# Softmax exponentials head by head from PSUM, with the scaled maximum as the bias

## The chip, the cores and the metric

The kernel runs on one core of a Trainium2 chip. The metric is the device time of one execution in microseconds (us); lower is better. The engines are called as the profile calls them: PE (TensorE), with PEld for its weight loads, DVE (VectorE), ACT (ScalarE), POOL (GpSimd) and SP (SyncE, which issues most of the transfers).

## The reference

The computation is a gated cross-attention block followed by a gated feed-forward block. There are 2 x 2048 rows of 512 numbers; each row attends to 77 context rows of its batch, with 16 heads of 32 numbers.

```python
x = x + tanh(g_xattn) * attention(layernorm(x), ctx)
x = x + tanh(g_ffn) * ffn(layernorm(x))
# attention, per head:
scores = q @ k.T / sqrt(32)              # 77 scores for each row
attn = softmax(scores, axis=-1)          # exp(scores - max) / sum
out = concat(attn @ v) @ Wo.T + bo
# ffn: two linear layers, each with its input and weight rounded to 127 levels
# by the largest absolute value of the whole tensor; an exact gelu between them
```

The change is inside the softmax: the largest of the 77 scores is taken from each of them, and the exponential is taken with the scale 1/sqrt(32).

## The kernel before, in words

The 4096 rows are cut into 8 blocks of 512 rows (index i). A block is worked on in 8 steps (index s), so attention has 64 steps, k = 8i + s. One step handles one group of four heads (g = s // 2) for two tiles of 128 rows; odd steps take the second pair of tiles. A step therefore owns 2 tiles x 4 heads x 77 = 616 scores in each of 128 partitions.

The stages of a step's softmax are these:

- `scores` (L342): eight matmuls write the 616 scores into the PSUM tile `ps` (two buffers). Each multiplies `qT`, the projected queries, with `kb`, the keys. DVE takes the maximum of each head's 77 scores into `mx` (L361), and subtracts it, from PSUM into the SBUF tile `e` (L363; three buffers).
- `exponential` (L371): one ACTIVATE on ACT, in place on the 616 numbers of `e` (L373).
- `shares` (L375): DVE sums each head (`sm`, L380) and inverts the sum (`rs`, L382); POOL multiplies `e` by it (L384).
- `transpose_a` (L388): PE transposes `e` into the PSUM tile `pta` (L395), and ACT copies it out as `aT` (L396).

Other work lies around it. `apply_v` (L398) multiplies with the values: PE writes `pc` (L404), ACT copies it to `cT` (L412). `project_q` (L329) makes the next queries: PE writes `pq` (L332), ACT makes `qT` from it (L340). `project_o` makes the output product `po` (L420), and DVE adds it to `x` (L430). `pq`, `pc`, `po` and a few others share two PSUM buffers (tag `pp`). DVE also takes the statistics of rows (L163, L164 and `ve`, L170) and maxima of normalised rows (L196, L445). POOL turns variances into `rstd` (L171), scales `xT` (L289) and adds the output bias to `x` (L327).

Preparation of the feed-forward weights is spread over the attention steps: maxima on DVE (`max_w`, L465) in steps 4 to 11 and 21 to 28; rounding on ACT (`raw_w`, L481) in steps 13, 15, 17, 19, 31, 32, 36 and 40; conversion on DVE (`w1q` and `w2q`, L489) one step after each.

In attention, the order on PE, DVE and ACT is exactly the order in which the program is written. In step k, PE does `apply_v` (even steps), the scores of step k + 2, the transposes of step k, then `project_o` (even) or `project_q` (odd). ACT does `cT` (even), two `aT` copies, the exponential of step k + 2, `qT` (odd), and then weight rounding. DVE does the output addition (odd), `mx` and the subtraction of step k + 2, row maxima or statistics (mostly even steps), `sm` and `rs` of step k + 2, further statistics (odd) and weight work. The core of the loop reads:

```python
if ahead[0] < NB:
    scores(*ahead)
for u in range(2):
    transpose_a(i, s, u)
...
if ahead[0] < NB:
    last = exponential(*ahead)
...
if ahead[0] < NB:
    last = shares(*ahead)
```

After attention comes a feed-forward part: gelu on ACT from the PSUM tile `ph` (L738, L746), and the second product `pf` (L805).

Of the kernel before, what the change touches and what calls it, by code (L numbers as in the profile page):

```python
# [8 lines left out]
F32 = mybir.dt.float32  # L9
BF16 = mybir.dt.bfloat16  # L10
AF = mybir.ActivationFunctionType
ALU = mybir.AluOpType
# [3 lines left out]
P = 128  # L16
# [4 lines left out]
NK = 77  # L21
HG = P // DK
NG = HEADS // HG
GK = HG * NK
RT = 2
NR = HG // RT
# [12 lines left out]
SCALE = float(DK) ** -0.5  # L39
# [3 lines left out]
def tile_flamingo_gated_block(  # L43
# [21 lines left out]
    nc = tc.nc  # L65
# [6 lines left out]
    small = ctx.enter_context(tc.tile_pool(name="small", bufs=4))  # L72
# [25 lines left out]
    work = actx.enter_context(tc.tile_pool(name="work", bufs=2))  # L98
# [106 lines left out]
    def quantize(dst, src, inv):  # L205

        nc.vector.tensor_scalar(src, src, inv, MAGIC, ALU.mult, ALU.add)
        return nc.vector.tensor_scalar(dst, src, MAGIC, None, ALU.subtract).ins  # L208
# [5 lines left out]
    with actx:  # L214
# [43 lines left out]

        rstd_row, po = {}, {}
        ALL = slice(0, D)  # L260
        ln, xnT, qT, aT, cT, es = {}, {}, {}, {}, {}, {}

        def norm_stats(i, t):

# [77 lines left out]
        def scores(i, s):  # L342

            g, half = divmod(s, 2)
            n = f"{i}_{s}"

            ps = ps_s.tile([P, NR, 512], F32, tag="ps", name=f"ps{n}")
            for u in range(2):
                t = 2 * half + u
                for q in range(NR):  # L350
                    r = slice(q * RT * DK, (q + 1) * RT * DK)
                    nc.tensor.matmul(  # L352
                        ps[:, q, u * RK : (u + 1) * RK],
                        qT[i, g][r, t * P : (t + 1) * P],
                        kblk[i // NBB][r, g, :],
                        start=True,
                        stop=True,
                    )
            mx = small.tile([P, NR, 2, RT], F32, tag="mx", name=f"mx{n}")
            sc = ps[:, :, : 2 * RK].rearrange("p q (u r k) -> p q u r k", u=2, r=RT)  # L360
            nc.vector.tensor_reduce(mx, sc, AX.X, ALU.max)  # L361
            e = work.tile([P, 2, GK], F32, tag="e", name=f"e{n}", bufs=3)
            nc.vector.tensor_tensor(  # L363
                e.rearrange("p u (q r k) -> p q u r k", q=NR, r=RT),
                sc,
                mx[:, :, :, :, None].to_broadcast([P, NR, 2, RT, NK]),
                ALU.subtract,
            )
            es[i, s] = e

        def exponential(i, s):  # L371
            e = es[i, s]
            return nc.scalar.activation(e, e, AF.Exp, scale=SCALE).ins  # L373

        def shares(i, s):  # L375

            n = f"{i}_{s}"
            e4 = es[i, s].rearrange("p u (j k) -> p u j k", j=HG)
            sm = small.tile([P, 2, HG], F32, tag="sm", name=f"sm{n}")
            nc.vector.tensor_reduce(sm, e4, AX.X, ALU.add)  # L380
            rs = small.tile([P, 2, HG], F32, tag="rs", name=f"rs{n}")
            nc.vector.reciprocal(rs, sm)  # L382
            es[i, s] = e4
            return nc.gpsimd.tensor_tensor(  # L384
                e4, e4, rs[:, :, :, None].to_broadcast([P, 2, HG, NK]), ALU.mult
            ).ins
# [152 lines left out]
        for s in range(2):  # L539
            scores(0, s)  # L540
            exponential(0, s)
# [4 lines left out]
        for i in range(NB):  # L546
            more = i + 1 < NB
            for s in range(2 * NG):
                g, odd = divmod(s, 2)
                k = i * 2 * NG + s  # L550
# [6 lines left out]
                if ahead[0] < NB:  # L557
                    scores(*ahead)
# [4 lines left out]
                if ahead[0] < NB:  # L563
                    last = exponential(*ahead)
# [22 lines left out]
                if ahead[0] < NB:  # L587
                    last = shares(*ahead)
# [44 lines left out]
        i, last = NB - 1, range(NG - 1, NG)  # L633
# [35 lines left out]
        for kc in range(0, KC, 2):  # L669
# [3 lines left out]
            last = nc.vector.tensor_scalar(xqT0[:, kc + 1, :], v, MAGIC, None, ALU.subtract).ins  # L673
# [23 lines left out]
    with ExitStack() as fctx:  # L697
# [23 lines left out]
        for i in range(NB):  # L721
# [4 lines left out]
            for a in range(GT):  # L726
                G = gtile(f"G{i}_{a}")
                for v in range(GF // 2):
# [16 lines left out]
                    for u, fc in chunks:  # L745
# [4 lines left out]
                            bias=b1s[:, fc : fc + 1],  # L750
                            scale=s1,
                        )
                    k = (i * GT + a) * 2 + v
                    n = 1 if k == NB * GT * 2 - 1 else 2
# [24 lines left out]
    for i in ends:  # L779
        hq = hpool.tile([P, FC, TB], BF16, tag="hq", name=f"hq{i}")  # L780
        for a in range(GT):
# [6 lines left out]
            if (i, a) == (first, 0):  # L788
                with tc.manual_schedule(engines={mybir.EngineType.DVE}):
                    for v in range(GF):  # L790
                        last = quantize(dst[:, v, :], G[:, v, :], inv_h)
# [25 lines left out]
        for t in range(NT):  # L817
# [3 lines left out]
            n = 2 if i == ends[-1] and t == NT - 1 else 1  # L821
            for j in range(n):
# [7 lines left out]
                r = i * TB + t * P  # L830
# [64 lines left out]
```

## Time and profile before

| what | value |
|---|---|
| median of 3 runs | 638.99 us (638.86 to 639.27) |
| the profiled execution | 640.32 us |
| its span on the core | 638.5 us |
| PE busy | 615.9 us, 96% of the span |
| DVE busy | 509.0 us, 80% |
| ACT busy | 341.0 us, 53% |
| POOL busy | 247.2 us, 39% |
| first scores on PE | 20.6 us after the start of the span |
| last attention exponential on ACT | 376.3 us |
| first feed-forward matmul | 404.9 us |

The span is the time between the first and the last instruction in the trace, and the execution's own time has some 1.8 us more around it. All durations below come from that one profiled execution. Busy shares are averages over parts with different limits, so they have to be read again for each part. Matmuls overlap in PE, so a busy PE isn't by itself a PE at its peak.

### The profile page before, as it was taken

The numbers are of one execution on the slowest core, as the hardware profiler recorded it, in microseconds if no ns is written. First come the engines' busy times: TensorE is split into PE (matmuls) and PEld (weight loads), VectorE is DVE, ScalarE is ACT, GpSimd is POOL, SyncE is SP. The second block draws the span as 40 slices with busy tenths as digits, with TensorE's granted clock in tenths as the row PEclk, the third lists the DMA queues.
The fourth block names the chain that finished last, engine by engine and source line by source line (L and its number), as shares of the span: only waits on it lengthen the run. The fifth ranks groups of instructions, "written<-read, shape, count | busy, mean of one in ns | idle before, by whom it ended". The sixth has DMA issues, their size and how long they took to land.

```text
span 638.5 us, 8087 instructions
## 1 busy us (share of the span) xinstructions
PE 615.9 (96%) x2957; PEld 311.5 (49%) x2978; DVE 509.0 (80%) x796; ACT 341.0 (53%) x450; POOL 247.2 (39%) x202
## 2 busy tenths in 40 slices
PE   5999999999999999999999999799999979999997
PEld 5556555455545554555545555344444424444444
DVE  5688777889898997887857787899999789877452
ACT  2255444563434654544344442598989879556510
POOL 2145457465355364273362341000000009998000
PEclk9999999999999999999999999799999989999999
DMA  9921510442520232220000000199999109798932
GB/s 282 371 97 52 119 42 26 114 168 78 136 66 1 84 131 67 82 68 2 16 1 1 1 17 0 51 337 302 346 331 294 20 24 380 271 376 315 399 129 82
DMA packets 50542, 90.66 MB, mean 142 GB/s; under 512 B 22139, under 2 KB 26491, under 8 KB 44872
## 3 DMA queue, kind: packets, MB, share of 16 engines
q1 hardware_dynamic: 49400, 89.48, 42.8%
q10 hardware_dynamic: 1104, 0.69, 0.4%
q8 instruction: 23, 0.38, 0.2%
q14 instruction: 15, 0.12, 0.1%
HBM read 55.01 MB, written 31.47 MB: 135 GB/s over the span
## 4 chain that ended last, share of the span: by engine, by line
PE 81%; DVE 15%; ACT 1%; POOL 1%; issue 1%; DMA 1%; DVEq 0%
PE ph L738 17%; PE pf L805 17%; PE po L420 13%; PE pq L332 13%; PE pta L395 8%; PE ps L352 6%; PE pc L404 4%; DVE e L363 2%; DVE mx L361 2%; DVE sm L380 1%; DVE st_a L163 1%; DVE max_w L465 1%; PE pk L226 1%; DVE xmax L445 1%; PE pvv L250 1%; DVE x L430 1%
## 5 line engine op out<-in xcount | busy, mean ns | idle before, releaser
L384 POOL TENSOR_TENSOR e<-e,rs 128x616 f32<-128x616 f32 x64 | 81.7, 1277 | 164.4 <-DVE rs L382 77.2
L396 ACT COPY aT<-pta 77x512 f32<-77x512 f32 x128 | 68.2, 583 | 99.4 <-PE pta L395 99.4
L420 PE MATMUL po<-wo_sb,cT 128*128 128x512 f32 (+1 forms) x264 | 115.1, 580 | 0.0
L805 PE MATMUL pf<-w2q,hq 128*128 128x512 bf16 (+1 forms) x518 | 112.0, 376 | 2.9 <-DVE hq L208 2.1
L738 PE MATMUL ph<-xqT,w1q 128*128 128x512 bf16 x501 | 112.0, 383 | 2.6 <-DVE xqT L208 1.8
L746 ACT ACTIVATE G<-ph,b1s,s 128x512 f32<-128x512 f32 x128 | 99.4, 777 | 13.8 <-PE ph L738 2.9
L332 PE MATMUL pq<-xT,wq_sb 128*128 128x512 f32 x192 | 86.6, 593 | 0.2 <-POOL xT L289 0.2
L756 DVE TENSOR_REDUCE hmax<-G 128x1 f32<-128x1024 f32 (+1 forms) x65 | 77.0, 1198 | 7.2 <-ACT G L746 7.1
L805 PEld LDWEIGHTS <-hq 128*128 128x128 bf16 x528 | 51.9, 99 | 62.9 <-DVE hq L208 3.0
L738 PEld LDWEIGHTS <-w1q 128*128 128x128 bf16 x512 | 50.6, 99 | 63.9 <-issue 4.9
L380 DVE TENSOR_REDUCE sm<-e 128x8 f32<-128x616 f32 x64 | 50.3, 787 | 25.9 <-ACT e L373 25.9
L420 PEld LDWEIGHTS po<-wo_sb,cT 128*128 128x128 f32 x264 | 47.8, 190 | 47.5 <-issue 46.2
L395 PE MATMUL pta<-ident,e 128*77 128x128 f32 x512 | 70.2, 280 | 0.6 <-POOL e L384 0.6
L373 ACT ACTIVATE e<-e 128x616 f32<-128x616 f32 x64 | 45.9, 718 | 44.2 <-DVE e L363 42.0
L361 DVE TENSOR_REDUCE mx<-ps 128x8 f32<-128x616 f32 x64 | 50.6, 791 | 17.2 <-PE ps L352 16.9
L395 PEld LDWEIGHTS pta<-ident,e 128*77 128x77 f32 x512 | 55.6, 147 | 11.4 <-issue 9.4
L798 ACT ACTIVATE Gb<-Gb,inv_h 128x2048 f32<-128x2048 f32 x22 | 43.6, 1999 | 32.4 <-DMA Gb<-h 32.4
L352 PEld LDWEIGHTS ps<-kb,qT 64*128 64x128 f32 x512 | 36.0, 186 | 46.9 <-ACT qT L340 23.1
L819 POOL TENSOR_TENSOR x<-x,b_sb 128x512 f32<-128x512 f32 x32 | 57.2, 1823 | 0.1
L363 DVE TENSOR_TENSOR e<-ps,mx 128x616 f32<-128x616 f32 x64 | 51.2, 800 | 6.7 <-DVE mx L361 0.5
L332 PEld LDWEIGHTS pq<-xT,wq_sb 128*128 128x128 f32 x192 | 34.5, 190 | 35.0 <-issue 33.5
L827 DVE SCALAR_TENSOR_TENSOR x<-pf,s,x 128x512 f32<-128x512 f32 (+1 forms) x33 | 23.7, 730 | 34.4 <-PE pf L805 28.4
(101 smaller groups left out, 666.2 us busy)
## 6 DMA issues: line engine op xcount, KB each, us to landing
h<-G SPq DMA_DIRECT2D x22, 1024.0 KB, 6.0
Gb<-h SPq DMA_DIRECT2D x22, 1024.0 KB, 7.9
out_y<-x SPq DMA_DIRECT2D x31, 256.0 KB, 3.2
x<-in_x SPq DMA_DIRECT2D x7, 1024.0 KB, 7.4
xT<-in_xT SPq DMA_DIRECT2D x6, 1024.0 KB, 5.5
raw_w<-in_w2T SPq DMA_DIRECT2D x6, 1024.0 KB, 5.5
raw_w<-in_w1T SPq DMA_DIRECT2D x4, 1024.0 KB, 12.5
rrow<-row SPq DMA_DIRECT2D x6, 256.0 KB, 4.8
```

The source lines that it names most:

```text
L332: nc.tensor.matmul(pq, wq_sb[:, kc, g * P : (g + 1) * P], (xnT if i < 2 else xT_sb)[i][:, kc, :], start=(kc == 0), stop=(kc == KC - 1),)
L352: nc.tensor.matmul(ps[:, q, u * RK : (u + 1) * RK], qT[i, g][r, t * P : (t + 1) * P], kblk[i // NBB][r, g, :], start=True, stop=True,)
L361: nc.vector.tensor_reduce(mx, sc, AX.X, ALU.max)
L363: nc.vector.tensor_tensor(e.rearrange("p u (q r k) -> p q u r k", q=NR, r=RT), sc, mx[:, :, :, :, None].to_broadcast([P, NR, 2, RT, NK]), ...
L384: return nc.gpsimd.tensor_tensor(e4, e4, rs[:, :, :, None].to_broadcast([P, 2, HG, NK]), ALU.mult).ins
L395: nc.tensor.transpose(pt[:NK, j, :], es[i, s][:, u, j, :], ident)
L396: nc.scalar.copy(aT[i, g][:, :, t * P : (t + 1) * P], pt[:NK, :, :])
L420: nc.tensor.matmul(po[i, t, c.start][:, : c.stop - c.start], cT[i, g][:, t * P : (t + 1) * P], wo_sb[:, g, c], start=(g == 0), stop=(g == ...
L738: nc.tensor.matmul(ph[u], w1q[:, kc, fc * P : (fc + 1) * P], cur[:, kc, :], start=(kc == 0), stop=(kc == KC - 1),)
L746: nc.scalar.activation(G[:, 2 * v + u, :], ph[u], AF.Gelu, bias=b1s[:, fc : fc + 1], scale=s1,)
L756: nc.vector.tensor_reduce(hmax[:, k + u : k + u + 1], G[:, 2 * v + u : 2 * v + u + n, :], AX.XY, ALU.max, apply_absolute_value=True,)
L805: nc.tensor.matmul(po[t, c.start][:, : c.stop - c.start], hq[:, fc, t * P : (t + 1) * P], w2q[:, fc, c], start=(fc == 0), stop=(fc == FC - 1),
```

## The change

The maximum is no longer subtracted by DVE. DVE multiplies `mx` by minus the scale instead (`nmx`, 128 x 8 numbers). ACT then reads the scores straight from PSUM: one ACTIVATE for each tile and head, eight per step, each over 77 numbers, with that head's column of `nmx` as the per-partition bias. It writes `e`, whose tile is now allocated in `exponential`. The place of every other instruction in its engine's order stays as it was.

```diff
-        ln, xnT, qT, aT, cT, es = {}, {}, {}, {}, {}, {}
+        ln, xnT, qT, aT, cT, es, scored = {}, {}, {}, {}, {}, {}, {}
...
             mx = small.tile([P, NR, 2, RT], F32, tag="mx", name=f"mx{n}")
             sc = ps[:, :, : 2 * RK].rearrange("p q (u r k) -> p q u r k", u=2, r=RT)
             nc.vector.tensor_reduce(mx, sc, AX.X, ALU.max)
-            e = work.tile([P, 2, GK], F32, tag="e", name=f"e{n}", bufs=3)
-            nc.vector.tensor_tensor(
-                e.rearrange("p u (q r k) -> p q u r k", q=NR, r=RT),
-                sc,
-                mx[:, :, :, :, None].to_broadcast([P, NR, 2, RT, NK]),
-                ALU.subtract,
-            )
-            es[i, s] = e
+            nmx = small.tile([P, NR, 2, RT], F32, tag="nmx", name=f"nmx{n}")
+            nc.vector.tensor_scalar(nmx, mx, -SCALE, None, ALU.mult)
+            scored[i, s] = sc, nmx
 
         def exponential(i, s):
-            e = es[i, s]
-            return nc.scalar.activation(e, e, AF.Exp, scale=SCALE).ins
+
+            sc, nmx = scored.pop((i, s))
+            es[i, s] = work.tile([P, 2, GK], F32, tag="e", name=f"e{i}_{s}", bufs=3)
+            for u in range(2):
+                for q in range(NR):
+                    for r in range(RT):
+                        j = q * RT + r
+                        last = nc.scalar.activation(
+                            es[i, s][:, u, j * NK : (j + 1) * NK],
+                            sc[:, q, u, r, :],
+                            AF.Exp,
+                            bias=nmx[:, q, u, r : r + 1],
+                            scale=SCALE,
+                        )
+            return last.ins
```

## The prediction

> **What bounds the kernel now.** I read engine shares first, then a table of engine time by stretch, then PE's waits, then the timeline.
>
> ```profile
> PE 615.9 (96%) x2957; PEld 311.5 (49%) x2978; DVE 509.0 (80%) x796; ACT 341.0 (53%) x450; POOL 247.2 (39%) x202
> ```
>
> The change touches attention only, some 20 to 378 us. By stretch (us, busy and instructions of PE, PEld, DVE, ACT, POOL, then clock, DMA):
>
> ```profile
> 30.00:72.00 42.00, 41.32 (x256) 24.93 (x255) 35.63 (x68) 23.69 (x46) 21.18 (x18) 1.00 0.36 99
> 72.00:127.00 55.00, 55.00 (x262) 28.20 (x260) 44.18 (x77) 26.40 (x41) 31.64 (x26) 1.00 0.26 64
> 127.00:197.00 70.00, 69.44 (x345) 35.03 (x344) 62.45 (x105) 32.07 (x51) 36.37 (x30) 1.00 0.37 106
> 260.00:375.00 115.00, 115.00 (x576) 59.36 (x572) 87.43 (x153) 48.56 (x81) 51.60 (x45) 1.00 0.08 23
> ```
>
> PE never rests, and successive pc products (L404) start 11.37 us apart (344.48, 355.85, 367.22): a pair of steps costs PE 11.37. A count of PE busy time says little, but these intervals show that the order on PE sets the pace. From 127 to 197 DVE is 89% busy and nearly ties. Freeing DVE can return only PE's waits in attention, about 1.6 us:
>
> ```profile
> PE ptx L323 <- DVE xn L314: 7.2, 2, 6.9
> PE pta L395 <- POOL e L384: 0.6, 2, 0.3
> PE ps L352 <- ACT qT L340: 0.4, 1, 0.4
> ```
>
> (The 7.2 lies before the first scores.) The third line is the narrow place. A query product pq ends an odd step, pc follows it for 1.0 us, and the next scores need the qT that ACT makes from pq in 0.69. In ACT's queue qT stands behind that odd step's exponential. So an exponential that ends over about 0.3 us after pq stalls PE. It happened once; ACT's timeline:
>
> ```profile
> 184.22 0.72 ACT L373 ACTIVATE e<-e 128x616 f32<-128x616 f32 x1 [2.80 <-DVE e L363]
> 184.85 0.67 ACT L340 ACTIVATE qT<-pq,bq_sb 128x512 f32<-128x512 f32 x1
> ```
>
> The scores due at 185.2 started at 185.57.
>
> **What the Trainium skill says.** "ScalarE: Activation LUTs", section What ACT_TABLE_LOAD costs: with a pointer bias an ACTIVATE takes about 280 ns + 0.833 per element, and back-to-back ones overlap by 93 ns. The trace agrees within 7%: 77 elements from PSUM with a pointer bias take 0.32 us (L242, page 0.344), qT 0.685 (page 0.707), and the pair 184.22/184.85 starts 0.09 inside the other.
>
> "SBUF — State Buffer", section SBUF: two separate sides: VectorE in a two-port mode and GpSimd share a port pair by an exclusive lock, held for a whole instruction. "VectorE: DVE Perf Modes", section Mode 2×_2P: tensor_scalar from SBUF can use that mode, PSUM sources can't. The trace agrees. DVE's small tensor_scalar:
>
> ```profile
> 155.19 0.17 DVE L170 TENSOR_SCALAR ve_a<-mv 128x4 f32<-128x4 f32 x1
> 162.28 0.60 DVE L170 TENSOR_SCALAR ve_f<-mean 128x2 f32<-128x2 f32 x1
> ```
>
> and POOL:
>
> ```profile
> 161.64 1.22 POOL L384 TENSOR_TENSOR e<-e,rs 128x616 f32<-128x616 f32 x1 [2.73 <-DVE rs L382]
> 134.27 1.99 POOL L384 TENSOR_TENSOR e<-e,rs 128x616 f32<-128x616 f32 x1 [4.99 <-PE ps L352]
> ```
>
> The smaller ve_f takes 0.60 and ends at 162.88, just after POOL's instruction at 162.86; the 1.99 stood against a w1q (L489) on DVE. After 92.05 a ve_f waited only for the POOL instruction under way, not for the next.
>
> **The change part by part.** These two groups go, 64 times each:
>
> ```profile
> L373 ACT ACTIVATE e<-e 128x616 f32<-128x616 f32 x64 | 45.9, 718 | 44.2 <-DVE e L363 42.0
> L363 DVE TENSOR_TENSOR e<-ps,mx 128x616 f32<-128x616 f32 x64 | 51.2, 800 | 6.7 <-DVE mx L361 0.5
> ```
>
> *ACT.* Eight 77-element ACTIVATEs replace one of 616: 0.32 + 7 x (0.32 - 0.09) = E = 1.92 us, +1.20 each, 77 us in all. Bounds: 2.10 with the page's prices, 2.6 without overlap, 1.8 if starts come faster. I take 1.92, from this trace. ACT's load in 260-375 grows from 42% to 60%: capacity is no bound, latency is.
>
> *DVE.* The subtraction's 0.72 of queue goes; the negation nmx (128x8) adds about 0.1, its result 0.2 after mx (as ve_a). With mx's 0.89 unchanged, the queue is 0.62 shorter. But nmx is a new two-port candidate: when POOL is mid-instruction it waits up to 1.27 (L327). The subtraction read PSUM and kept 0.80 throughout. Bounds on this cost: 0 and 1.27; I take it where POOL's present instructions cover nmx's new place.
>
> *Latency.* mx to exponential's end was 0.89+0.80+0.03+0.72 = 2.44; it becomes 0.89+0.20+1.92 = 3.0, up to 4.2 with the lock. Behind it in ACT's queue: qT (then PE), weight rounding raw_w, copies cT and aT. On DVE the sum sm waits for it; behind sm stand output addition, statistics and the next mx.
>
> *At no cost.* PSUM ps is now freed by ACT, not DVE, but its buffer is wanted two steps (11.4 us) later and the exponential ends some 4.2 us after the scores; were that cover gone, the full +0.56 would count. e has three buffers. No DMA or queue position moves; eight ACTIVATEs stand in the old one's place and nmx in the subtraction's.
>
> *Where it is hidden.* Steady odd step of 260-375, zero at the end of its scores: the preceding even exponential starts behind the aT copies and ends near -1.6; sm, rs, mx put nmx ready at +0.9. By then POOL runs x (L327, 1.27) behind e, so nmx ends near +2.2 and the exponential at +4.15. pq ends at 4.45, so qT's limit is +4.7: 0.5 to spare, no cost.
>
> *Start, 29-72.* Steps are short. In step 1, nmx is ready at 35.1 but POOL's e covers it to 35.6; the exponential ends at 37.6, qT at 38.2; scores started at 36.83: +1.4. By step 3 qT is 2.8 late (47.7 for 44.9), and pc, which needs one of two PSUM buffers that qT's source holds, stalls to about +1.9. In steps 5-6 the exponential ends at 59.2 and qT at 59.85; pc began at 57.09: +2.8 in all (2.0 without lock).
>
> *Weight rounding, steps 13-21.* A ring closes from one odd exponential's end to the next: qT 0.60, raw_w 1.90, cT 0.47, aT 1.00, E 1.92, gap 0.03, sm 0.82, rs 0.12, w1q 1.09, output addition 0.66, mx 0.89, nmx 0.20 + lock 0.70 (w1q delays POOL's e, x or xT stands over nmx), E 1.92 = 12.32 against PE's 11.37. Four pairs x 0.95, less 0.5 of slack on entry: +3.3. Without lock 11.62: +0.5.
>
> *Weight maxima, steps 21-29.* DVE's ring: gap, sm, rs, statistics 0.77, maximum 1.10, mx = 3.73; then to the even sm 2.46 where normalisation fills the wait, else 0.20+1.92+0.03 = 2.15; then sm, rs, maximum 1.09, addition 0.66, mx, nmx, E = 5.70. Pairs: 11.58, 12.40 (with ve_f, 0.51), 11.89, 12.79 (ve_f and a lock of 0.70): excess 3.2. The present stalls there, 0.6, are in it: net +2.6. The saved 0.62 and the longer wait nearly cancel: a present pair here lasts 12.0 to 12.6 on DVE but enters with slack.
>
> *Second rounding, steps 31-33:* one ring, +0.5. *Tail:* step 62's e comes 0.4 earlier and PE's wait of 0.33 at 375.56 goes: -0.3. The last DVE chain has 2.4 us of idle at 389 to absorb 1.4.
>
> Sum: 2.8+3.3+2.6+0.5-0.3 = **+8.9**. The profiled execution took 640.32 (span 638.5 and 1.8 around); the median is 638.99, 1.3 below. 640.3+8.9 = 649.2 profiled, about **648** as median.
>
> **Rivals.**
> - *The lock does not bite* (nmx too small for the mode, or it falls between POOL's instructions): 2.0+0.5+1.9-0.3 = +4.1, **643**. Against it: ve_f with 2 elements is held. Chance 0.25.
> - *Dearer exponentials*, E about 2.1 to 2.3: eight DVE or rounding pairs pay twice 0.18 to 0.38, the start and second rounding some 1.3 to 2.5 more, and over 2.25 the steady slack of 0.5 ends: **652 to 657**. Chance 0.15. At 2.6 without overlap the sixteen light pairs lose 2 x 0.68 - 0.5 = 0.9 each as well: about **680**, chance 0.03; the overlap in every pair of aT copies speaks against it.
> - *DVE's relief wins.* One mechanism: in 127-197, where the DVE chain leads, 0.62 per step returns before sm is waited for. Price: at most PE's 1.6 us of waits: **637.5**. It decides if E falls under about 1.3, where an odd step's mx-to-sm is no longer than today's. Nothing shows that. Faster by over 0.2%: 0.05.
> - *All is absorbed*: slack covers the start too, **639**; speaking against it is the 0.3 left to qT. Chance 0.07.
> - That the edit does not happen is excluded: the changed kernel's order shows eight ACTIVATEs per stage and no subtraction.
>
> **How the numbers follow.** My case has 0.45: 648. A measurement tells about 0.2% (1.3 us) from no change. Slower 0.25+0.45+0.15+0.03 = 0.88. The range 642 to 657 takes in the lock-free case and the dearer exponentials.
>
> **What would show it.** L374's ACTIVATEs about 320 ns each and 1.9 us per eight; DVE busy down some 40 us; nmx with a mean well over 0.17, odd ones ending with POOL; PE waits ps<-qT and pc<-qT of some 8 us, in 36-60 and 110-200, none after 250; pc 11.37 apart after 250. I am wrong if E is far from 1.92, if stalls fall in the steady part, or if the first 72 us keep their length.

## The result, and the profile after

| | before | after |
|---|---|---|
| median | 638.92 us (638.42 to 639.27) | 654.58 us (653.24 to 656.01) |
| ratio to before | 1 | 1.0246 (95% interval 1.0218 to 1.0274) |
| profiled execution, span | 640.32, 638.5 us | 655.66, 653.9 us |

The kernel became 15.7 us slower; 648 was forecast, with 657 as the upper end. The direction held, and so did the mechanism but for the steady part; the size was short by some 6.6 us. The busy shares of the engines (after) show little of that. DVE lost 13 us of busy time and ACT gained 66, and PE is still the fullest engine:

```profile
PE 619.2 (95%) x2957; PEld 312.9 (48%) x2978; DVE 495.9 (76%) x796; ACT 407.5 (62%) x898; POOL 246.1 (38%) x202
```

The stretches of attention again (after; same columns as in the prediction, PE to POOL busy, then the clock):

```profile
30.00:72.00 42.00, 38.46 (x227) 24.13 (x226) 30.65 (x64) 29.07 (x93) 19.55 (x16) 0.96 0.33 100
72.00:127.00 55.00, 53.31 (x262) 27.10 (x261) 38.05 (x72) 36.07 (x105) 29.99 (x25) 1.00 0.19 36
127.00:197.00 70.00, 66.81 (x331) 33.73 (x330) 55.23 (x100) 43.04 (x131) 32.36 (x26) 1.00 0.36 118
260.00:375.00 115.00, 113.15 (x560) 57.99 (x559) 85.19 (x155) 71.64 (x225) 51.82 (x45) 1.00 0.11 33
```

Before, PE had no idle time in the second and fourth stretch; now it has holes in all four. The first one also shows a clock of 0.96. The waits of PE (after: total us, times, longest) say who makes the holes:

```profile
PE ps L352 <- ACT qT L340: 8.6, 12, 1.2
PE pc L412 <- ACT qT L340: 1.9, 2, 1.4
PE pq L332 <- POOL xT L289: 1.2, 1, 1.2
PE pq L332 <- DVE nmx L363: 1.1, 1, 1.1
```

qT accounts for 10.5 us in fourteen waits, where before it was 0.4 in one. The third and fourth lines are the same kind of wait: PE wants POOL's scaled xT. The fourth is put down to DVE, but in POOL's own timeline xT ran from 204.97 to 206.23, and PE's product began at 206.29.

The two groups that stand behind qT (after, groups by line):

```profile
L374 ACT ACTIVATE e<-ps,nmx 128x77 f32<-128x77 f32 x512 | 116.9, 343 | 57.9 <-DVE nmx L363 57.8
L363 DVE TENSOR_SCALAR nmx<-mx 128x8 f32<-128x8 f32 x64 | 35.3, 552 | 2.2
```

Eight ACTIVATEs in a row take 1.83 us in the timeline (343 ns each, 212 from start to start). The negation takes 171 ns at its shortest, 552 on average and 1282 at the longest: 33 of the 64 take 171 to 173 ns, and each of the other 31 ends 0.03 us after an instruction of POOL ends. Odd steps average 822 ns, even ones 281. Its waiting is counted as busy, and this is why DVE's busy time fell by only 13 us.

Where the time went is read from the starts of the transposes on PE, eight records for each of the 64 steps; the first of them marks the step. For each stretch of steps, the table gives by how many us a kernel fell behind the kernel before. "All" runs from the first transposes to the last, because the time up to the first ones differs by itself (29.7 us in this profile of the changed kernel, 27.5 in another):

| kernel | steps 0-13 | 13-21 | 21-33 | 33-45 | 45-63 | all |
|---|---|---|---|---|---|---|
| forecast, my case | 2.8 | 3.3 | 2.6 | 0.5 | 0 | 9.2 |
| after | 4.5 | 3.4 | 3.4 | 3.7 | 0 | 15.0 |

(The second rounding's 0.5, forecast for steps 31 to 33, is put under 33-45, where its stall fell.)

### The profile page after: what moved, and what is told of

Read it like the earlier page. It is cut to its first block, busy times and chain, and to the rows that moved or that the text cites. A ratio compares the mean times of both kernels' runs of the same rounds, so it can differ in the third digit from the quotient of the medians.

```text
span 653.9 us, 8634 instructions
## 1 busy us (share of the span) xinstructions
PE 619.2 (95%) x2957; PEld 312.9 (48%) x2978; DVE 495.9 (76%) x796; ACT 407.5 (62%) x898; POOL 246.1 (38%) x202
## 4 chain that ended last, share of the span: by engine, by line
PE 60%; DVE 25%; ACT 11%; issue 2%; DMA 1%; POOL 1%; DVEq 0%; ACTq 0%
PE pf L813 17%; PE ph L746 16%; ACT e L374 8%; PE pq L332 7%; PE po L428 7%; PE pta L403 5%; DVE sm L388 4%; PE ps L352 3%; DVE mx L361 3%; DVE nmx L363 3%; DVE x L438 2%; PE pc L412 2%; DVE xmax L453 2%; DVE st_f L163 2%; DVE max_w L473 2%
## 5 line engine op out<-in xcount | busy, mean ns | idle before, releaser
L374 ACT ACTIVATE e<-ps,nmx 128x77 f32<-128x77 f32 x512 | 116.9, 343 | 57.9 <-DVE nmx L363 57.8
L352 PE MATMUL ps<-kb,qT 64*128 64x154 f32 x512 | 51.2, 319 | 8.7 <-ACT qT L340 8.6
L804 POOL TENSOR_SCALAR b_sb<-b_sb,s 128x512 f32<-128x512 f32 x1 | 3.5, 3496 | 121.7 <-issue 121.7
```

Source lines behind the costliest of these rows:

```text
L352: nc.tensor.matmul(ps[:, q, u * RK : (u + 1) * RK], qT[i, g][r, t * P : (t + 1) * P], kblk[i // NBB][r, g, :], start=True, stop=True,)
L374: last = nc.scalar.activation(es[i, s][:, u, j * NK : (j + 1) * NK], sc[:, q, u, r, :], AF.Exp, bias=nmx[:, q, u, r : r + 1], scale=SCALE,)
```

## The experiments

Two causes were in the change together: longer exponentials, and a negation that waits for the port that DVE shares with POOL. The runs undo one of them, or both, or part of the steps. Each kernel is compared with the kernel before on the same chip, whose median lay between 639.1 and 640.3 us. Losses in stretches or in attention come from one profile of each kernel; they can differ from the loss in the median by up to some 2 us.

**The old way in block 0.**

```diff
+            if i == 0:
+                e = work.tile([P, 2, GK], F32, tag="e", name=f"e{n}", bufs=3)
+                nc.vector.tensor_tensor(e.rearrange(...), sc, mx[...].to_broadcast(...), ALU.subtract)
+                es[i, s] = e
+                return
...
+            if i == 0:
+                e = es[i, s]
+                return nc.scalar.activation(e, e, AF.Exp, scale=SCALE).ins
```

> The scores of block 0 alone go the old way (subtraction on DVE, one exponential of 616); the other seven blocks stay changed. My theory: of the 15.7 us lost, 4.6 are lost before step 8, some 2.8 of them because qT stands behind a longer exponential in short steps, and some 1.8 because TensorE's clock dipped to half after a stall of 1.4 us; both go, so about 650 us, with the clock at 1.00 between 55 and 75 us and the later losses as they were. Rival: the clock dip comes at that time whatever PE does; then about 652. Second rival: the loss is spread evenly over the steps (8 of 64 steps, 2 us): 652.6.

Measured: 650.56 us (650.03 to 650.99). The start lost 0.0 instead of 4.5 us, the clock was 1.00 from 55 to 75 us, and the later stretches lost what they had lost (3.7, 3.6, 3.3). So the start is worth 4 to 4.5 us, and an even spread over the steps is out.

**No port wait: the negation reads PSUM.**

```diff
-            mx = small.tile([P, NR, 2, RT], F32, tag="mx", name=f"mx{n}")
+            mx = ps[:, :, 320:324].rearrange("p q (u r) -> p q u r", u=2)
```

> The maxima mx are kept in spare columns of the PSUM tile, so the negation reads PSUM instead of SBUF; everything else as changed. My theory: the negation's mean of 552 ns (171 when free) is the wait for a port that POOL holds for a whole instruction, and a PSUM source does not need it: all 64 negations under 0.3 us, and the stalls that the lock adds go; the lock-free sum of the prediction gives about 643, up to 647 if a clock dip stays. Rival: the eight exponentials alone (1.83 us for 0.72) make the loss and the lock only moves waits about: 652 to 654.

Measured: 644.26 us, ratio 1.0073 (1.0058 to 1.0088). The negation's group in this kernel:

```profile
L363 DVE TENSOR_SCALAR nmx<-ps 128x8 f32<-128x8 f32 x64 | 10.7, 166 | 2.2
```

The mean went from 552 to 166 ns, with the same instruction count, the same exponentials and the same order; the maximum itself took 800 ns against 790. Of the 15.7 us lost, 4.8 are left in the median, and of the 15.0 in attention 4.6. So the wait of the negation is shown to be the larger part of the loss. In steps 33 to 45 this kernel loses nothing.

**One exponential, negation kept.**

```diff
+            return nc.scalar.activation(es[i, s].rearrange(...), sc, AF.Exp,
+                                        bias=nmx[:, 0, 0, 0:1], scale=SCALE).ins
```

> One ACTIVATE of 616 from PSUM takes the place of the eight, with the bias of one head for all (the other heads' maxima are left out of the exponential); negation with its port wait stays. My theory: from mx to the end of the exponential is 0.83 + 0.17 to 1.28 + 0.78 = 1.8 to 2.9 us against 2.44 before, so PE's stalls go but for a few odd steps: 638 to 641. If the port wait by itself is what costs: 645 or more. If DVE's relief can win more than PE's few waits: under 637.

Measured: 638.04 us, ratio 0.998 (0.9969 to 0.999). The exponential takes 778 ns, the negation is still 483 ns on average, and attention is 1.2 us shorter than before. So here, with a short exponential and no subtraction, the port wait costs nothing, and DVE's relief is worth less than the 1.6 us of PE's waits that the forecast set as its ceiling.

**No negation, eight exponentials.** The reduction negates, and the scale is in the keys; `bks_sb`, the scaled bias of the keys, is made once, at the start.

```diff
+            nc.vector.tensor_reduce(mx, sc, AX.X, ALU.max, negate=True)
-            nmx = small.tile([P, NR, 2, RT], F32, tag="nmx", name=f"nmx{n}")
-            nc.vector.tensor_scalar(nmx, mx, -SCALE, None, ALU.mult)
...
+    nc.gpsimd.tensor_scalar(bks_sb, bk_sb, SCALE, None, ALU.mult)
```

> The scale is put into the keys and the reduction negates the maximum itself, so no negation is left on DVE; eight exponentials stay. My theory: as the kernel with the maxima in PSUM, less 0.1 to 0.2 us in each step: 642 to 646, with the remaining loss in the start and in steps 13 to 29. Rival (eight exponentials alone): 652 to 654.

Measured: 646.12 us, just above the range, for a reason of its own. My line on POOL's queue held up the first rows' `rstd`: PE's wait for the first normalised rows grew from 7.2 to 10.3 us, and the first transpose of attention weights came 4.7 us late. From there to the last it lost only 2.0 us. The same kernel with that line on DVE in step 0:

> As the kernel without negation, but the scaled key bias is made by DVE in step 0 instead of at the head of POOL's queue, where it held up the first rows' statistics by 3 us and more. That kernel lost 2.0 us between its first and its last attention transpose against the kernel before; so 641 to 642. Rival: the loss at the start was not that queue: 646.

Measured: 640.91 us, ratio 1.0021 (1.0001 to 1.004). Eight exponentials cost 0.6 us in the median and 2.0 in attention if no negation stands in front of them. So neither the long exponentials alone nor, as the kernel with one exponential and no subtraction showed, the negation alone makes the loss.

**The negation added to the kernel before.**

```diff
             nc.vector.tensor_reduce(mx, sc, AX.X, ALU.max)
+            nmx = small.tile([P, NR, 2, RT], F32, tag="nmx", name=f"nmx{n}")
+            nc.vector.tensor_scalar(nmx, mx, -SCALE, None, ALU.mult)
```

> The kernel before, with the negation of the maxima added on DVE ahead of the subtraction (its result is not used); exponentials as before, one of 616. Theory, as it stands after four runs: the port wait costs only where qT's slack is used up, and with the short exponential there are 2 us of it; the added 0.1 to 1.2 us on DVE falls hardest in steps 21 to 29, where DVE was level with PE: 639 to 642. Rival: each wait for the port is paid in full (64 x 0.4 = 25 us, or half of it in odd steps): 650 or more.

Measured: 648.36 us, ratio 1.0138 (1.0118 to 1.0158). The expectation missed. Here the exponential is 0.72 us, as before, and still 9.2 us are lost in the median and 7.0 in attention. The subtraction is also still there, so mx to the end of the exponential is long again, and DVE has more to do than in any other kernel (534.0 us busy, 509.0 before). The exponential's length alone is thus not the quantity. Whether the whole interval or DVE's queue makes these 7.0 us was not separated.

**Four exponentials of 154.**

> Four ACTIVATEs of 154 in place of eight of 77 (each pair of heads gets one head's bias, the other head's maximum is left out); negation with its port wait stays. By the eight's start-to-start of 212 ns and 343 ns each, four take 0.41 + 3 x 0.28 = 1.24 us. Theory: there is a slack of qT to be used up, so the loss is no straight line between one (638.0 at 0.78 us) and eight (654.6 at 1.83): 639 to 643. Rival: a straight line in the time of the exponentials: 645.3.

Measured: 638.16 us, ratio 0.9984 (0.9974 to 0.9994); four in a row take 1.23 us. A straight line between one and eight would have given 645.3: the loss begins only somewhere between four and eight.

**The maxima in PSUM in odd steps only.**

```diff
+            if s % 2:
+                mx = ps[:, :, 320:324].rearrange("p q (u r) -> p q u r", u=2)
```

> The maxima lie in PSUM in odd steps only; even steps negate from SBUF and wait for the port. Theory: only in odd steps does qT stand behind the exponential, and the long port waits were in odd steps; so this is within 1.5 us of the kernel with all maxima in PSUM: 643.5 to 646. Rival: the waits of even steps count as much, by delaying the whole DVE queue: halfway, 649.

Measured: 645.91 us (644.98 to 647.21), near the 644.26 of all steps. Freeing the odd steps, in which qT follows the exponential, brings most of it: 8.8 us of attention, where freeing all steps brings 10.4. The negations left on SBUF, those of even steps, average 265 ns here.

**The late weight conversions left out.** Three quarters of the second weight matrix stay at zero in this kernel, so only the times of attention are used.

> The changed kernel without the weight conversions of steps 33, 37 and 41 (those three quarters of the second weight matrix are left at zero, written by a fill in steps 49, 51 and 53 where DVE has time). Theory: in steps 33 to 45 the stalls come because each of these conversions stands 1.77 to 2.08 us in DVE's queue and makes the next odd step's maximum 1.8 us late, on top of a negation that waits out a whole POOL instruction; so of the 3.7 us lost between steps 33 and 45 at most 1.0 stays, and the rest of attention is as it was; about 651 to 652 if the second product takes its time as before. Rival: the port wait alone makes those stalls, in every third step of a block: 3.7 stays.

Measured: 651.24 us. From step 33 to step 45 it lost 0.7 us instead of 3.7; the stretches 13-21 and 21-33 lost 3.8 and 3.5. So a conversion (L497 after) starts each of the later stalls, in two moves that the changed kernel's timelines show around step 43. DVE:

```profile
281.17 1.77 DVE L497 TENSOR_SCALAR w2q<-raw_w 128x2048 bf16<-128x2048 f32 x1
282.86 0.79 DVE L361 TENSOR_REDUCE mx<-ps 128x8 f32<-128x616 f32 x1
...
287.67 0.79 DVE L361 TENSOR_REDUCE mx<-ps 128x8 f32<-128x616 f32 x1
288.50 1.28 DVE L363 TENSOR_SCALAR nmx<-mx 128x8 f32<-128x8 f32 x1
```

POOL:

```profile
288.48 1.26 POOL L289 TENSOR_TENSOR xT<-xT,rrow 128x512 f32<-128x512 f32 x1
```

ACT:

```profile
289.87 1.83 ACT L374 ACTIVATE e<-ps,nmx 128x77 f32<-128x77 f32 x8 [2.21 <-DVE nmx L363]
291.54 0.74 ACT L340 ACTIVATE qT<-pq,bq_sb 128x512 f32<-128x512 f32 x1
```

PE:

```profile
290.36 1.06 PE L412 MATMUL pc<-aT,vb 77*32 77x512 f32 x8
292.33 0.80 PE L352 MATMUL ps<-kb,qT 64*128 64x154 f32 x8 [0.91 <-ACT qT L340]
```

The conversion makes the maximum at 282.86 late, and the next one at 287.67 starts 1.7 us after its scores (their PE work ended at 285.96). The negation comes 0.02 us after POOL began xT and ends just after it. The exponential then ends at 291.7, after pq's end at 290.4, and qT is late by 0.91 us. In the kernel before, these three conversions took 1.77 to 1.78 us and cost nothing. It takes both: with the maxima in PSUM the conversions took 1.77 to 2.07 us and steps 33 to 45 lost nothing, and in the changed kernel negations of 1.28 us without a conversion before them (at 252.3 and 276.1) made no hole on PE.

**A filler in PE's longest wait**, in `project_k`.

```diff
-            for kc in range(KC):
+            for kc in [*range(KC)] * (2 if (b, g) == (1, 2) else 1):
```

> The changed kernel with one key product (eight matmul records, 0.85 us on PE) done twice, in the place where PE waits 1.41 us for qT in step 6; nothing else changes. Theory: the clock's dip to half at 61 us follows that wait; with the wait down to some 0.5 us the dip goes, and the kernel is 1.5 to 2 us faster though it does more work on PE: 652.5 to 653. Rival: the dip has nothing to do with the wait: no change, 654.6.

> The changed kernel once more, beside the one with the filler on the same chip. Its four first times lay in two pairs, 653.2 to 653.5 and 655.7 to 656.0. Theory: the difference is the dip of the clock near 61 us, which some executions have: again two groups some 2 us apart, and a profile with a span near 651.5 shows no dip. Rival: ordinary scatter, with times in between.

Measured on one chip: 653.08 us with the filler (652.53 to 654.72), 654.03 without (653.49 to 654.72). The ranges overlap, so the times don't decide it, and the two groups of times did not come again; the second profile of the changed kernel shows the dip. The traces say more. Two stretches of the changed kernel, then the same of the kernel without late conversions, which has the same wait of 1.4 us; the third number from the end is the granted clock (before DMA share and GB/s):

```profile
58.00:60.00 2.00, 0.70 (x7) 0.55 (x5) 0.49 (x1) 2.00 (x8) 0.00 (x0) 1.00 0.00 0
62.00:64.00 2.00, 2.00 (x11) 1.69 (x10) 1.94 (x4) 0.79 (x2) 1.19 (x1) 0.50 0.00 0
```

```profile
58.00:60.00 2.00, 1.00 (x10) 0.17 (x10) 1.15 (x3) 1.26 (x4) 0.36 (x1) 1.00 0.00 0
62.00:64.00 2.00, 2.00 (x10) 1.10 (x10) 1.93 (x5) 1.76 (x8) 0.09 (x1) 1.00 0.15 8
```

The dip lasts 3.4 us, from 61.0 to 64.4. Three profiles have the wait of 1.4 us: two show the dip, one does not. From step 5 to step 8 they lose 2.8 and 2.9 us with it, and 1.25 without. The profiles of the kernels in which this wait is shorter (0.8 us or less: maxima in PSUM, filler, block 0 the old way) show no dip there. So a dip costs about 1.6 us and comes in some executions after that wait. That the wait causes it is likely and not proven: the cases are few.

**A version below both.** One maximum for the four heads of a tile (it cancels in the softmax as any common bias does, as long as no head's own maximum lies so far below the common one that its exponentials vanish), two ACTIVATEs of 308, no subtraction and no negation:

```diff
+            mx = small.tile([P, 2], F32, tag="mx", name=f"mx{n}")
+            nc.vector.tensor_reduce(mx, sc.rearrange("p q u r k -> p u q (r k)"),
+                                    AX.XY, ALU.max, negate=True)
...
+                last = nc.scalar.activation(es[i, s][:, u, :].rearrange(...),
+                                            sc[:, :, u, :, :], AF.Exp, bias=nmx[:, u : u + 1])
```

> A candidate to beat both: the maximum is taken over the four heads of a tile together (128x2, negated by the reduction, scale in the keys), so two ACTIVATEs of 308 do, some 0.9 us, with no negation and no subtraction. Theory: mx to the end of the exponential is about 0.85 + 0.9 = 1.75 us against 2.44 before, PE's waits in attention go, and PE's order is the floor: 636.5 to 638.5, that is 0.1 to 0.4% under the kernel before. Rival: DVE's shorter queue (0.7 us in 64 steps) is worth more than PE's waits: under 634.

Measured: 637.76 us, ratio 0.9975 (0.9966 to 0.9984). Its groups:

```profile
L375 ACT ACTIVATE e<-ps,mx 128x308 f32<-128x308 f32 x128 | 59.3, 519 | 5.1 <-DVE mx L365 4.9
L365 DVE TENSOR_REDUCE mx<-ps 128x2 f32<-128x616 f32 x64 | 50.8, 795 | 28.9 <-PE ps L356 28.5
```

DVE now waits 28.5 us in all for PE's scores, where the changed kernel waited 2.2. In attention 0.6 us of PE's waits are left. The end is PE's own order, and the gain stops at a quarter of a per cent.

**The runs side by side.** Attention's loss against the interval from the start of mx to the end of the exponential, added up from each kernel's means (0.83 to the negation, its mean, 0.80 of the subtraction, the exponentials, 0.03):

| kernel | interval, us | 0-13 | 13-21 | 21-33 | 33-45 | all |
|---|---|---|---|---|---|---|
| two of 308, no negation | 1.8 | -0.5 | 0 | -0.9 | 0 | -1.4 |
| one of 616 | 2.1 | -0.6 | 0.3 | -0.9 | 0 | -1.2 |
| before | 2.4 | 0 | 0 | 0 | 0 | 0 |
| four of 154 | 2.6 | -0.5 | 0.1 | -0.9 | 0 | -1.3 |
| eight, no negation (mended) | 2.7 | 1.3 | 1.0 | -0.3 | 0 | 2.0 |
| eight, maxima in PSUM | 2.9 | 1.8 | 1.4 | 1.5 | 0 | 4.6 |
| negation added to before | 2.9 | 0.6 | 0.5 | 2.9 | 2.9 | 7.0 |
| eight, odd maxima in PSUM | 2.9 | 1.8 | 1.8 | 2.6 | 0 | 6.2 |
| after | 3.2 | 4.5 | 3.4 | 3.4 | 3.7 | 15.0 |

Up to 2.6 us the interval is free; 0.6 more costs 15 us. Read from the timelines of odd steps, with the times that ACT itself comes late, it is 2.44 us on average before, 2.86 with four, 3.00 with eight and no negation, and 3.60 after. Kernels with equal means still lose between 4.6 and 7.0 us. They differ in where their long waits fall and in how long DVE's queue is, but which of these makes the difference was not tested. The mean is a guide, not a law.

## Why the prediction was right, and where it was short

- **PE's order is the floor.** Right: the three lightest kernels gained 1.2 to 1.4 us in attention against a ceiling of 1.6, and pc starts are 11.37 us apart from step 46 to step 60.
- **qT behind the odd exponential is the narrow place.** Right: 10.5 us of PE's waits, of "some 8" forecast.
- **E = 1.92.** Measured 1.83. Starts are 212 ns apart where I took 230; the overlap was 131 ns, not 90. Slightly too dear, the wrong way for the shortfall. ACT's load from 260 to 375 us came to 62% (71.64 of 115), where the forecast had 60; its own prices, 1.20 us for each of some 20 steps there, give 63.
- **The lock on the port.** Right, as the deciding term. "Steady" negations of 1.03 to 1.28 us are in the trace from 299 us on and cost nothing there, as forecast. The rival without the lock gave 643, that is 4.1 us more than before; the kernel with its maxima in PSUM measured 644.26, 4.8 more.
- **Start, 2.8.** Measured 4.5. The stalls were there and in the forecast's places (step 1 to 2: 1.2 at 38.1; after steps 3 and 5: 0.5 at 47.4 and 1.4 at 60.1, on pc). The missing 1.6 is the half clock that follows the wait, which was in no case of mine: the two kernels with the same start but without the dip (the filler, and no late conversions) lost 3.0 there. "TensorE: Matmul & The Clock Gate", section Part 1: The HAM clock gate, says that the array falls to half clock after an idle window of about 3.4 us, and that the window runs freely. The half clock agrees with the 0.50 above; but the wait here was 1.4 us, in a stretch where PE was still 74% busy (3.70 of 5 us, 55 to 60). So for this kernel the measurement decides: the clock fell without an idle window of that length. What made it fall is not shown.
- **Weight rounding, 3.3.** Measured 3.4, partly for another reason, so the close match is luck: 1.2 of it is one wait for xT (at 109.5 us), which leaves 2.2 against the ring's 3.3. POOL does `e` before xT in its queue, `e` comes later because the sums do, and POOL had been full since 100.9 us:

```profile
107.01 1.23 POOL L392 TENSOR_TENSOR e<-e,rs 128x616 f32<-128x616 f32 x1
108.18 1.27 POOL L289 TENSOR_TENSOR xT<-xT,rrow 128x512 f32<-128x512 f32 x1
109.51 1.13 PE L332 MATMUL pq<-xT,wq_sb 128*128 128x512 f32 x2 [1.20 <-POOL xT L289]
```

I had followed DVE and ACT behind the exponential, but not POOL behind the sums. The same happens at 206.3 us, for 1.1.

- **Weight maxima, 2.6, and second rounding, 0.5.** In steps 21 to 33 it measured 3.4, of which that second xT wait is 1.1, so 2.3 are left for the 2.6; the second rounding's stall of 0.6 came at step 34.
- **"No cost" in the steady part.** This step failed, by the forecast's own sign, which was stalls in the steady part and waits after 250 us. I had worked out one clean odd step, with DVE on time, and found 0.5 us to spare. Steps 33 to 45 have weight conversions in them, and 3.0 us were lost there besides the second rounding, mostly in waits of 0.9 us at 244.9, 268.6 and 292.3. Each conversion takes the 0.5 away before the negation comes. The kernel without these conversions lost 0.7 there in all, which is the rounding's part.
- **DVE's busy time "down some 40 us".** Wrong by my own terms: a wait for the port is counted as busy, and 64 of them average 552 ns. It fell by 13.
- **Tail, -0.3.** Nothing came of it.
- **The upper end, 657.** 654.58 lies in the range that was priced for dearer exponentials, 652 to 657, but at 1.83 us for eight they were cheaper than assumed. That rival did not come true, so that the time still fell inside the range is in part luck: the half clock and the conversions, which no case had, filled the room that was left for it.

The shortfall of 5.8 us in attention (15.0 for 9.2) is thus the half clock (1.6, in the profiled execution), the conversions (3.0), and POOL's queue behind the sums (2.3; by arithmetic only 0.9 of it shows, and the rest lies inside ring terms that were too dear). The remaining 0.3 is spread over the start and the second rounding.

## What to carry to other kernels

Count what stands behind an instruction in its engine's queue, and how much slack that has: here a slack that the forecast put at 0.3 to 0.5 us decided, while every engine but PE had about a quarter or more of its time free. A tiny instruction can cost more than the large one it replaces if it has to wait out another engine's instructions: here 0.17 us of work took up to 1.28 us, where the subtraction that it replaced took 0.80. A source in PSUM, or letting the reduction do the negation, took that cost away. When a part is called steady, take its worst step, not its cleanest.

## What the runs showed of the hardware

- A negation of 8 numbers in each partition took 171 ns free and up to 1282 ns while POOL was in an instruction that lasts 1.26 us; each of the 31 longer ones ended 0.03 us after a POOL instruction. From PSUM it took 166 on average and 168 at most. This agrees with the exclusive lock of "SBUF — State Buffer", section SBUF: two separate sides, on an instruction whose own work is negligible.
- ACTIVATEs of 77 with a pointer bias started 212 ns apart, each 343 ns long; of 154, four took 1.23 us. "ScalarE: Activation LUTs", section What ACT_TABLE_LOAD costs, would give an estimate of 251 ns between starts of the former.
- The clock fell to 0.50 for 3.4 us after a PE wait of 1.4 us, in two profiles of three that had such a wait.
